# Row statistics of a layer norm inside a state-space scan: ScalarE accumulated sums in place of VectorE's statistics instructions

## The chip, the cores and the metric

The kernel runs as one program on one core of a Trainium2 chip. The metric is the device time of one launch in microseconds (us); lower is better. In the trace the engines are called PE (TensorE, with its weight loads as PEld), DVE (VectorE), ACT (ScalarE), POOL (GpSimd) and SP (SyncE, which only issues transfers here).

## What is computed

A two-layer network over 4096 tokens of width 256: graph convolution with a Mamba block, a mixture of experts, a second graph convolution, a second mixture of experts. Only the first graph convolution and its Mamba block are touched by the change:

```python
h = jax.nn.relu(adj @ x @ gcn_w + gcn_b)
mu = h.mean(-1, keepdims=True)
var = h.var(-1, keepdims=True)
h = (h - mu) * lax.rsqrt(var + EPS) * ln_g + ln_b      # the input norm
xz = h @ w_in                                          # 4096 x 1024: xc and z
u = silu(causal_conv4(xc)); dt, B, C from u            # 512 channels, 16 states
def step(hst, inp):                                    # over the 4096 tokens
    hst = dAt * hst + dBut
    return (hst, hst @ Ct)
y = (ys + u * D_skip) * silu(z);  out = y @ w_out
```

## The kernel before

**The scan stage.** The tokens are cut into 8 chunks of 512 (`CW`), a chunk into 4 tiles of 128 rows (`TPC`). The scan is written out by hand as 32 steps per chunk (`STEPS`); a step takes one block of 128 channels and two of the 16 states. The order in which the instructions are issued is each engine's order of execution; an engine never overtakes. In step n:

- POOL multiplies `db` for step n+1 (`inputs`, L1103) and then issues the accumulating transfer that adds the two halves of step n-1's `hc` (`pair`, L1132). `db` has two buffers, so the multiply for step n+1 needs step n-1's product on DVE and its state copy on ACT to be finished.
- DVE runs two scans (L1118), each on one decay `da` that ACT has made one step ahead (`decay`, L1111), and then the product `hc = db * cb` (L1128).
- ACT copies the last column of the state (L1124), and PE adds older `hc` into `psy` (L1145).

**The front of the next chunk.** From step 8 of chunk c on, the work ahead of chunk c+1's scan is slipped into the steps: `Front.PLAN` names what follows the product of a step, `Front.EARLY` what comes between the scans and the product. Chunk 0's front runs ahead of the scan, alone. The front's input norm is spread so:

| Step | Function | Engine and line before |
|---|---|---|
| 8 | `do_gcn` | PE L700 |
| 9 | `do_biased` | DVE adds the bias (L707), ACT takes the Relu, 128x512 at a time (L711) |
| 10, early | `do_stats` | DVE: four `bn_stats` (L715) and four `bn_aggr` (L716) |
| 10, early | `do_root` | DVE adds EPS (L719), POOL raises to the power -1/2 (L720) |
| 11 | `do_normal` | DVE makes `-mean * rstd` (L723), ACT normalises, four tiles (L727) |
| 12 | `do_turn` | PE transposes (L735) |
| 13 | `do_turned`, `do_xz` | ACT copies out with gain and bias (L742), PE multiplies by `w_in` (L754) |
| 17 | `do_silu` | ACT, after PE's convolution (L771), takes the Silu (L781) |

**The propagation pieces.** `adj @ x` for chunk c+2 (L642) is cut into 66 pieces per chunk (64 of matmuls, and two copies of the result, L648). A small loop ahead of the scan gives each step a number of pieces: it keeps an estimate of PE's time and of DVE's time per step (`PE_COST`, `DVE_COST`) and puts each next piece where PE's estimate is lowest against DVE's.

**The same statistics elsewhere.** While chunk 6 and 7 are scanned, `Tail.put` and `Tail.squares` take the row sums of the block's output by ACT: an Identity with a summed output (L905), the negated mean (L915) and a Square with the mean as bias and a summed output into `junk` (L919). `Norm.root` (L932, L935) and `Norm.shift` (L941) turn them into scale and shift.

Of the kernel before, what the change touches and what calls it, by code (L numbers as in the profile page):

```python
# [9 lines left out]
F32 = mybir.dt.float32  # L10
BF16 = mybir.dt.bfloat16
I32 = mybir.dt.int32
AF = mybir.ActivationFunctionType
ALU = mybir.AluOpType
# [4 lines left out]
P = 128  # L19
CW = 512  # L20
TPC = CW // P
TR = 256
EPS = 1e-5
# [5 lines left out]
def kernel(ctx: ExitStack, tc: tile.TileContext, out: bass.AP, **a):  # L29
    nc = tc.nc  # L30
    x, adj, adjT = a["x"], a["adj"], a["adjT"]
    N, D = x.shape
# [16 lines left out]
    small = ctx.enter_context(tc.tile_pool(name="small", bufs=3))  # L49
# [489 lines left out]
    with ExitStack() as s1:  # L539
# [51 lines left out]
        junk = ra.tile([P, D], F32, name="junk")  # L591
# [26 lines left out]
        FILL = {11: 8, 12: 2, 16: 1, 18: 2, 20: 2, 21: 6, 22: 1, 24: 40}  # L618
        PIECE, PE_STEP, DVE_STEP = 1.0, 1.1, 4.3
        PE_COST = {"gcn": 2, "turn": 0.8, "xz": 2, "conv": 4, "project": 2, "dt": 1}  # L620
        DVE_COST = {"biased": 0.8, "stats": 1.4, "soft": 2.7}
        psts, fronts = {}, {}
        
        def propagation(c):
# [27 lines left out]
        class Front:  # L652
# [3 lines left out]


            PLAN = {
                8: ["gcn 0", "gcn 1"], 9: ["biased 0", "biased 1"], 11: ["normal"],
                12: ["turn 0", "turn 1"], 13: ["turned 0", "turned 1", "xz 0", "xz 1"],  # L660
                14: ["in 0", "in 1", "xz 2"], 15: ["conv 0", "in 2"], 16: ["conv 1"],
                17: ["silu 0", "conv 2"], 18: ["xz 3"], 19: ["in 3", "project 0"],
# [4 lines left out]
                38: ["in 7"], 39: ["silu 2"],  # L667
            }
            EARLY = {
                10: ["stats 0", "stats 1", "root"], 27: ["soft 0"], 29: ["soft 1"],  # L670
                30: ["soft 2"], 31: ["soft 3"],
            }

            def __init__(self, c):
                self.c = c
                self.pts = psts.pop(c)
                self.h = w1p.tile([P, TPC, D], F32, name="h", tag="h")
                self.st = small.tile([P, TPC, 6], F32, name="ln_st")
                self.mv = small.tile([P, TPC, 2], F32, name="ln_mv")
                self.rs = small.tile([P, TPC], F32, name="ln_rs")  # L680
                self.nm = small.tile([P, TPC], F32, name="ln_nm")
                self.ps, self.psy = {}, {}
# [22 lines left out]
            def do_biased(self, hh):  # L705
                hs = self.h[:, 2 * hh:2 * hh + 2, :]
                nc.vector.tensor_tensor(  # L707
                    hs, self.ps.pop(("gcn", hh)), gcn_b.unsqueeze(1).to_broadcast([P, 2, D]),
                    ALU.add,
                )  # L710
                nc.scalar.activation(hs, hs, AF.Relu)  # L711

            def do_stats(self, hh):
                for t in range(2 * hh, 2 * hh + 2):
                    nc.vector.bn_stats(self.st[:, t, :], self.h[:, t, :])  # L715
                    nc.vector.bn_aggr(self.mv[:, t, :], self.st[:, t, :])  # L716

            def do_root(self):
                nc.vector.tensor_scalar(self.rs, self.mv[:, :, 1], EPS, None, ALU.add)  # L719
                nc.gpsimd.tensor_tensor(self.rs, self.rs, mhalf[:, :TPC], ALU.pow)  # L720

            def do_normal(self):
                nc.vector.scalar_tensor_tensor(  # L723
                    self.nm, self.mv[:, :, 0], -1.0, self.rs, ALU.mult, ALU.mult
                )
                for t in range(TPC):
                    nc.scalar.activation(  # L727
                        self.h[:, t, :], self.h[:, t, :], AF.Identity, bias=self.nm[:, t:t + 1],
                        scale=self.rs[:, t:t + 1],
                    )  # L730
# [425 lines left out]
        with tc.manual_schedule(engines={  # L1156
# [6 lines left out]
            for i, names in [*Front.PLAN.items(), *Front.EARLY.items()]:  # L1163
                for name in names:
                    pe[i % STEPS] += PE_COST.get(name.split()[0], 0.0)
                    dve[i % STEPS] += DVE_COST.get(name.split()[0], 0.0)
            pieces = [0] * STEPS
# [503 lines left out]
```

## Time and profile before

| | |
|---|---|
| Median of 3 runs | 2469.72 us (2467.38 to 2470.41) |
| The profiled execution, its own time | 2471.36 us |
| Its span, first to last instruction | 2469.6 us |
| Mean granted clock of PE | 0.955 |
| Busy share of the span: PE, DVE, ACT, POOL | 91%, 67%, 48%, 46% |
| The scans' first and last start | 168.7 us and 1288.7 us |

The span holds several stages one after the other: the first norm of x, chunk 0's propagation and front, the scan stage (some 1120 us), routing, the first experts, the second graph convolution, the second experts. The busy shares are means over all of them, so what a change inside the scan stage is worth is read from rows of that stage. In the timelines below a row gives start, duration, engine, line, operation, what it writes and reads, and, in brackets, how long the engine sat idle before it and who ended that.

### The profile page before, as it was taken

The page shows a single profiled execution, that of the slowest core. Times are in us where ns is not written, and L with a number is a line of the kernel's source. Part 1 is how long each engine was busy: PE and PEld are TensorE (multiplying, and loading weights), DVE is VectorE, ACT ScalarE, POOL GpSimd, SP SyncE. Part 2 cuts the span into 40 slices and gives each one's busy share as a digit, 9 for nine tenths or more (in the row PEclk, how much of TensorE's full clock was granted, in tenths as well). Part 3 has the DMA queues.
Part 4 walks back from the last instruction along what each step waited for, and adds up shares of the span by engine and source line. Part 5 has one row for each costly group of instructions (what it writes and reads, how often), then busy time and mean ns, then how long its engine had stood idle before and what let it go on. Part 6 is the DMA issues. An engine that isn't in the chain of part 4 may idle for free. (4 is left out here: it accounts for less than half of the span.)

```text
span 2469.6 us, 27703 instructions
## 1 busy us (share of the span) xinstructions
PE 2258.3 (91%) x8984; PEld 1635.7 (66%) x8984; DVE 1657.0 (67%) x2376; ACT 1180.8 (48%) x2013; POOL 1141.7 (46%) x830
## 2 busy tenths in 40 slices
PE   5989989999999989997994999969999999989985
PEld 4765655646565655643663888857788888878874
DVE  4049999999999999989897111165466666744233
ACT  1136657465655657466662322224555555633321
POOL 1027777687777677776551455410000000036652
PEclk9989999999999999997995999989999999999998
DMA  6359998989999999988655777643344444447886
GB/s 205 94 160 245 239 271 219 270 225 273 228 249 263 237 266 225 273 235 217 210 184 171 237 229 234 216 162 109 103 146 149 149 145 145 143 137 235 248 278 228
DMA packets 290364, 509.46 MB, mean 206 GB/s; under 512 B 25232, under 2 KB 157456, under 8 KB 289312
## 3 DMA queue, kind: packets, MB, share of 16 engines
q1 hardware_dynamic: 243936, 410.54, 53.2%
q0 software_dynamic: 46272, 97.03, 18.2%
q8 instruction: 75, 1.23, 0.2%
q14 instruction: 81, 0.66, 0.1%
HBM read 406.03 MB, written 42.73 MB: 182 GB/s over the span
## 5 line engine op out<-in xcount | busy, mean ns | idle before, releaser
L1103 POOL TENSOR_TENSOR db<-du,bb 128x1024 f32<-128x1024 f32 x256 | 607.2, 2372 | 357.5 <-ACT state L1124 130.0
L1118 DVE TENSOR_TENSOR_SCAN db<-da,state,db 128x512 f32<-128x512 f32 x512 | 627.2, 1266 | 44.6 <-ACT da L1111 42.3
L642 PE MATMUL pt<-at,gn 128*128 128x256 f32 x2048 | 489.6, 391 | 34.0 <-DMA at<-in_adjT_dram 27.1
L1111 ACT ACTIVATE da<-dt,negA 128x512 f32<-128x512 f32 x512 | 347.8, 691 | 357.0 <-DVE db L1118 355.3
L642 PEld LDWEIGHTS pt<-at,gn 128*128 128x128 f32 x2048 | 398.4, 196 | 164.0 <-issue 73.6
L1398 PE MATMUL pf<-gn,f 128*128 128x256 f32 x2048 | 452.0, 380 | 0.0
L1398 PEld LDWEIGHTS pf<-gn,f 128*128 128x128 f32 x2048 | 386.6, 190 | 57.2 <-issue 6.4
L1128 DVE TENSOR_TENSOR hc<-db,cb 128x1024 f32<-128x1024 f32 x256 | 331.4, 1294 | 17.9
L1145 PE MATMUL psy<-hc,ident 128*128 128x512 f32 x576 | 304.9, 622 | 41.9 <-DMA hc<-hc 33.4
L79 POOL TENSOR_TENSOR ln_rs<-ln_rs,mhalf 128x4 f32<-128x4 f32 x24 | 34.0, 1416 | 512.1 <-DVE ln_rs L78 512.1
L460 DVE TENSOR_TENSOR yk<-ps_y,bk 128x512 f32<-128x512 f32 x73 | 50.4, 691 | 326.5 <-PE ps_y L455 280.8
L1387 ACT ACTIVATE f<-f 128x1024 f32<-128x1024 f32 x128 | 134.5, 1057 | 197.8 <-DVE f L1386 133.8
L470 PE MATMUL ps_h<-xkT,wk 128*128 128x256 f32 x864 | 213.8, 389 | 11.7 <-DVE xkT L495 6.3
L455 PE MATMUL ps_y<-wk,hk 128*128 128x256 f32 x864 | 211.0, 381 | 0.1
L1132 POOL DMA_DIRECT2D hc<-hc x224 | 195.4, 873 | 0.2
L470 PEld LDWEIGHTS ps_h<-xkT,wk 128*128 128x128 f32 x864 | 160.2, 194 | 45.8 <-ACT hk L474 13.5
L1145 PEld LDWEIGHTS psy<-hc,ident 128*128 128x128 f32 x576 | 110.5, 198 | 120.3 <-issue 59.0
L1386 DVE TENSOR_SCALAR f<-at 128x1024 f32<-128x1024 f32 x128 | 88.1, 688 | 149.3 <-PE pf L1398 135.9
L455 PEld LDWEIGHTS ps_y<-wk,hk 128*128 128x128 f32 x864 | 161.6, 191 | 21.6 <-ACT hk L474 0.9
L474 ACT ACTIVATE hk<-ps_h,d_b 128x256 f32<-128x256 f32 x140 | 66.2, 474 | 184.0 <-PE ps_h L470 184.0
L1393 DVE SCALAR_TENSOR_TENSOR cnt<-at,cnt 128x1024 bf16<-128x1024 f32 x120 | 145.8, 1215 | 9.8 <-DMA at<-in_adjT_dram 8.9
L754 PE MATMUL ps_xz<-hT,w_in 128*128 128x512 f32 x256 | 124.9, 623 | 12.9 <-ACT hT L742 12.9
(305 smaller groups left out, 2568.8 us busy)
## 6 DMA issues: line engine op xcount, KB each, us to landing
at<-in_adjT_dram SPq DMA_DIRECT2D x256, 512.0 KB, 4.4
bb<-bcd SPq DMA_DIRECT2D x128, 512.0 KB, 5.1
cb<-bcd SPq DMA_DIRECT2D x128, 512.0 KB, 4.9
hc<-hc POOLq DMA_DIRECT2D x224, 256.0 KB, 6.7
wk<-in_L_ffn_W_dram SPq DMA_DIRECT2D x70, 512.0 KB, 5.2
wk<-in_L_ffn_expert_w_dram SPq DMA_DIRECT2D x114, 256.0 KB, 4.3
yg<-d_ys SPq DMA_DIRECT2D x16, 512.0 KB, 4.1
yd<-us SPq DMA_DIRECT2D x6, 1024.0 KB, 7.8
```

Source lines behind the costliest of these rows:

```text
L455: nc.tensor.matmul(ps[:, j, :], hT[:, m, j * P:(j + 1) * P], w[:, m, :], start=(m == 0), stop=(m == kb_out - 1),)
L470: nc.tensor.matmul(ps[:, j, :], w[:, d, m * P:(m + 1) * P], xT[:, d, :], start=(d == 0), stop=(d == DB - 1),)
L642: nc.tensor.matmul(pt[:, k, :], xl[:, j, k * P:(k + 1) * P], at[:, jj, :], start=(j == 0 and k == 0), stop=(j == NT - 1 and k == DB - 1),)
L1103: nc.gpsimd.tensor_tensor(self.db, self.f.du[self.half][:, self.mi:self.mi + 1, :].to_broadcast([P, 2, CW]), self.bb, ALU.mult,)
L1111: nc.scalar.activation(da, self.f.dt[self.half][:, self.mi, :], AF.Exp, scale=negA[:, self.m, n:n + 1])
L1118: nc.vector.tensor_tensor_scan(self.db[:, j, :], da, self.db[:, j, :], state[:, self.m, n:n + 1], ALU.mult, ALU.add,)
L1128: nc.vector.tensor_tensor(self.hc, self.db, self.cb, ALU.mult)
L1132: nc.gpsimd.dma_start(self.hc[:, 0, :], self.hc[:, 1, :], accum_op=ALU.add)
L1145: nc.tensor.matmul(f.psy[m], ident, self.hc[:, j, :], start=False, stop=(self.g == GS - 1 and j == last),)
L1387: nc.scalar.activation(f, f, AF.Square)
L1393: nc.vector.scalar_tensor_tensor(cnt, at, 0.0, cnt, ALU.is_gt, ALU.add)
L1398: nc.tensor.matmul(pf[:, t, :], f[:, jj, t * P:(t + 1) * P], gn[:, j, :], start=(j == 0 and t % 2 == 0), stop=(j == NT - 1 and t % 2 == 1),)
```

## The change

The variance and mean that `bn_stats` and `bn_aggr` made on DVE are made by summed outputs on ACT. `do_biased` splits its Relu into four, one per 128-row tile, each with a summed output into `nm`. `do_stats` moves from early in step 10 to the end of step 10: ACT turns the sums into negated means and takes four Squares with summed outputs into `rs`. `do_root` moves from early in step 10 to early in step 11, and its DVE instruction now also scales by 1/D. `do_normal` stays at the end of step 11; its DVE instruction becomes a plain multiplication of two tiles. The entry "stats" leaves `DVE_COST`; by the loop's arithmetic step 10 then gets 3 pieces of the propagation in place of 5, and steps 26 and 28 get 3 in place of 2.

```diff
-        DVE_COST = {"biased": 0.8, "stats": 1.4, "soft": 2.7}
+        DVE_COST = {"biased": 0.8, "soft": 2.7}
...
-                8: ["gcn 0", "gcn 1"], 9: ["biased 0", "biased 1"], 11: ["normal"],
+                8: ["gcn 0", "gcn 1"], 9: ["biased 0", "biased 1"], 10: ["stats"], 11: ["normal"],
...
             EARLY = {
-                10: ["stats 0", "stats 1", "root"], 27: ["soft 0"], 29: ["soft 1"],
+                11: ["root"], 27: ["soft 0"], 29: ["soft 1"],
...
-                self.st = small.tile([P, TPC, 6], F32, name="ln_st")
-                self.mv = small.tile([P, TPC, 2], F32, name="ln_mv")
...
-                nc.scalar.activation(hs, hs, AF.Relu)
-
-            def do_stats(self, hh):
                 for t in range(2 * hh, 2 * hh + 2):
-                    nc.vector.bn_stats(self.st[:, t, :], self.h[:, t, :])
-                    nc.vector.bn_aggr(self.mv[:, t, :], self.st[:, t, :])
+                    nc.scalar.activation(
+                        self.h[:, t, :], self.h[:, t, :], AF.Relu, accum_out=self.nm[:, t:t + 1]
+                    )
+
+            def do_stats(self):
+                nc.scalar.activation(self.nm, self.nm, AF.Identity, scale=-1.0 / D)
+                for t in range(TPC):
+                    nc.scalar.activation(
+                        junk, self.h[:, t, :], AF.Square, bias=self.nm[:, t:t + 1],
+                        accum_out=self.rs[:, t:t + 1],
+                    )

             def do_root(self):
-                nc.vector.tensor_scalar(self.rs, self.mv[:, :, 1], EPS, None, ALU.add)
+                nc.vector.tensor_scalar(self.rs, self.rs, 1.0 / D, EPS, ALU.mult, ALU.add)
                 nc.gpsimd.tensor_tensor(self.rs, self.rs, mhalf[:, :TPC], ALU.pow)

             def do_normal(self):
-                nc.vector.scalar_tensor_tensor(
-                    self.nm, self.mv[:, :, 0], -1.0, self.rs, ALU.mult, ALU.mult
-                )
+                nc.vector.tensor_tensor(self.nm, self.nm, self.rs, ALU.mult)
```

## The prediction

> **What bounds the kernel now.** I read the page's busy slices first, then the waits of the scan stage, then the timelines of steps 10 and 11 of one chunk. The slices:
>
> ```profile
> PE   5989989999999989997994999969999999989985
> DVE  4049999999999999989897111165466666744233
> ACT  1136657465655657466662322224555555633321
> ```
>
> In slices 3 to 20, the scan stage, PE and DVE are both at 9 and ACT at 4 to 7, so two engines could be the bound. The waits of DVE from 306 to 1152 us (six chunks) decide it:
>
> ```profile
> DVE db L1118 <- ACT da L1111: 29.0, 22, 2.8
> DVE us L1154 <- PE psy L1145: 3.9, 2, 2.1
> ```
>
> DVE waits 33 us in 846, and for PE hardly at all. A plain step is two scans and a product on DVE, and the next scan starts 3.68 us later (357.51 to 361.19 below). PE does idle: 0.70 us before the transposes of step 12 and 2.90 us before step 14's `xz` in this chunk. So DVE's queue sets the pace, and an instruction in it costs its full length. Steps 10, 11 and 12 of chunk 1, as the table of windows shows them (length first, then each engine's busy time):
>
> ```profile
> 347.31:353.12 5.81, 5.81 (x26) 4.63 (x25) 5.64 (x13) 2.23 (x5) 3.16 (x3) 1.00 1.04 246
> 353.12:357.51 4.39, 4.39 (x17) 2.87 (x16) 4.30 (x5) 1.50 (x3) 4.16 (x3) 1.00 0.92 282
> 357.51:361.19 3.68, 2.49 (x13) 1.72 (x13) 3.59 (x6) 3.39 (x7) 3.17 (x2) 1.00 0.84 215
> ```
>
> Step 10 is 2.13 us over a plain step, step 11 is 0.71 over. The timelines of DVE and POOL say why:
>
> ```profile
> 351.25 0.39 DVE L715 BATCH_NORM_STATS2 ln_st<-h 128x6 f32<-128x256 f32 x1
> 351.68 0.18 DVE L716 BATCH_NORM_AGGREGATE ln_mv<-ln_st 128x2 f32<-128x6 f32 x1
> 351.90 0.17 DVE L719 TENSOR_SCALAR ln_rs<-ln_mv 128x4 f32<-128x4 f32 x1
> 351.98 1.22 DVE L1128 TENSOR_TENSOR hc<-db,cb 128x1024 f32<-128x1024 f32 x1
> ...
> 355.66 1.85 DVE L1128 TENSOR_TENSOR hc<-db,cb 128x1024 f32<-128x1024 f32 x1
> ```
> ```profile
> 352.16 1.94 POOL L720 TENSOR_TENSOR ln_rs<-ln_rs,mhalf 128x4 f32<-128x4 f32 x1 [2.65 <-DVE ln_rs L719]
> 354.08 2.35 POOL L1103 TENSOR_TENSOR db<-du,bb 128x1024 f32<-128x1024 f32 x1
> ```
>
> The statistics fill step 10. The power delays POOL's `db` to 354.08; it ends at 356.43, and step 11's product, which reads two tiles as POOL's multiply does, takes 1.85 us in place of 1.22 and ends 1.08 after it. The power, too, needs 1.94 us beside a product (it ends 0.90 after the product's 353.20) and 1.01 us in chunk 0's front, where DVE is idle. So these two engines hold each other up, and the order in which they start counts.
>
> **The change, part by part.** I follow step 10 of chunk 1 with its scan's start as zero.
>
> *Removed from DVE:* eight instructions and the first `root`, in all 2.13 us. Step 10 falls from 5.81 to 3.68, and POOL's `db` for step 12 starts at 3.92 (product's end 3.76 plus 0.16, as in other steps) and ends at 6.26, before step 11's product: the 0.63 us of contention goes as well.
>
> *Added to ACT:* the rows of the same operations in the tail:
>
> ```profile
> 1062.62 0.21 ACT L915 ACTIVATE x_mean<-x_sum 128x2 f32<-128x2 f32 x1
> 1062.86 0.51 ACT L919 ACTIVATE junk<-xr,x_mean 128x256 f32<-128x256 f32 x1
> 1063.27 0.19 ACT L919 ACTIVATION_READ_ACCUMULATOR junk<-xr,x_mean 128x1 f32 x1
> 1063.49 0.51 ACT L919 ACTIVATE junk<-xr,x_mean 128x256 f32<-128x256 f32 x1
> ```
>
> A Square comes every 0.63 us, since the next writes the same `junk`. ACT's state copy of step 10 starts at 3.10 as before (the four Relus end near 1.3, where the decays first have to wait for a scan anyway). Then the mean at 3.19, Squares at 3.43, 4.06, 4.70 and 5.33, the last sum at 5.93. Queued behind them are the decays for step 12; the first could start at 4.96 and starts at 5.9. They end at 7.2 and are needed after 7.4: hidden, by 0.2 us if nothing else were late.
>
> *Moved: `root`.* On DVE it stands behind step 11's scans, at 6.04. The sums are there at 5.93, so no wait, but `db` is on POOL until 6.26; row L932, the same form, took 0.23 us in that place. The product then runs from 6.22 to 7.45. On POOL the power is moved past step 10's accumulating transfer, which holds POOL's queue for 0.87 us (6.24 to 7.12). It starts at 7.12 beside the product and ends 0.88 after it, at 8.33.
>
> *The new wait.* `normal`'s multiplication on DVE now waits for that power; behind it in DVE's queue stand step 12's scans, and so everything. DVE idles from 7.45 to 8.37. Worse, POOL's `db` for step 13 needs only step 11's product and state copy (7.27), so it starts as soon as the power is off POOL: at 352.16 + 1.94 = 354.10 against 354.08 above, 0.02 us before the power's end. DVE starts 0.04 after a power that it waits for (chunk 0's front: power at 92.99 for 1.01, L723 at 94.04). So `db` is first by some 0.05 us, and what a small DVE multiplication of two tiles does beside it, the last chunk shows:
>
> ```profile
> 1161.60 2.33 POOL L1103 TENSOR_TENSOR db<-du,bb 128x1024 f32<-128x1024 f32 x1
> ```
> ```profile
> 1161.75 2.21 DVE L941 TENSOR_TENSOR x_shift<-x_mean,x_dev 128x12 f32<-128x12 f32 x1
> ```
>
> It ends 0.03 after POOL's. So `nm` ends at 8.31 + 2.35 + 0.03 = 10.69, and step 12's scan starts at 10.61 (0.08 ahead of the end, as at 357.51). Steps 10 and 11 take 10.61 in place of 5.81 + 4.39 = 10.20: +0.41 us a chunk, for the seven chunks that carry a front +2.9 us. The bounds: with `nm` first, the scan starts at 8.33 + 0.04 + 0.15 - 0.08 = 8.44, or -1.76 a chunk (-12.3 in all); with the sums 0.5 us late, +0.9 a chunk (+6.4). Lateness is the smaller doubt; between the two orders the row at 0.15 us speaks for the blocked case, but it is a row at 0.15 and not at 0.05.
>
> The Trainium skill (SBUF — State Buffer, § Who interferes with whom) says that a VectorE instruction with two SBUF inputs and a GpSimd one that reads SBUF share an interface, that "Issue order, not op shape, decides who blocks", and that the loser waits for the whole instruction. The 2.21 us row agrees; the rule alone would give the blocked case, +2.9 us, and it speaks against this change.
>
> *Chunk 0's front* has nothing to hide behind. Today `nm` starts at 94.04, ACT normalises from 94.29 to 96.36, and PE, which has pieces until 96.5, loses nothing. The Relu of the second half starts at 90.55; as two with sums it lasts until 91.48 (0.42 from start to start: half of L711's 512 columns in 0.33, the sum 0.09), the mean until 91.72, the Squares until 94.22, `root` until 94.5, the power (1.01) until 95.5, `nm` until 95.7: ACT normalises from about 95.85, 1.55 us later. PE loses 1.15 of it, as the first transposes can start on the first tiles. PE then sets the way to the scan's start: +1.15 us (0.3 to 1.6).
>
> *The propagation pieces.* Two of the five leave step 10, and one each joins steps 26 and 28. A piece is four matmuls, 0.9 us. PE is up to 1.3 us later at the copy in step 28 where its idle time there is 0.46 us. ACT may wait that long, but the decays behind the copy are 3.9 us early in a step with the softplus work. PE catches up in step 2, where it waits 1.2 to 3.6 us for `hc`. I cost it at nothing; without that cover it is 1.3 us in three chunks, +4.
>
> *The sum:* -2.13 x 7 = -14.9 in step 10; step 11 from 4.39 to 6.93, +2.54 x 7 = +17.8; front 0 +1.15; together +4.1 us. The profiled execution, 2471.36, becomes 2475.4; the median of the runs is 1.64 below it, so 2473.8.
>
> **The rivals.** *`nm` gets in first.* The 0.05 us lie inside the gap that no row shows: -12.3 + 1.15 = -11.2, 2458.6 us. For it: POOL's power in its first 0.13 us does not yet collide (1.01 alone, 0.88 after a product), so its start is not quite its claim. Against: DVE's blocked product shows the same 0.15.
>
> *The granted clock of PE.* PE's idle time before the transposes grows from 0.70 to about 2.3 us, as it has two pieces less and `nm` comes no earlier. In chunk 1 the 2.90 us of idle time before `xz` cost it: the clock in 364 to 370 us is 0.73 and 0.70, the second Silu of step 18 waits for PE, and the step's scans start 5.80 us apart (379.67 and 385.47) against 4.29 in chunk 2, where the slow stretch fell elsewhere. Four of seven chunks pay this today (1, 3, 5, 6). If the other three pay too, +1.5 x 3 = +4.5, 2478.3 us. It decides when the clock is below 1 over `xz` in every chunk. The Trainium skill (TensorE: Matmul & The Clock Gate, Part 1) gives free-running windows of 3.4 us, of which an idle one halves the clock; a 2.3 us gap would by that rule be enough in some chunks and not in others, and the sum would lie between the two.
>
> *It makes no difference in the scan*, because PE would have held DVE back anyway: then only front 0 counts, 2470.9. The 3.9 us in the waits speak against it.
>
> **How the numbers follow.** Blocked `nm` 0.56, with a range of its own of 2470 to 2479 (sums late, clock by chance); `nm` first 0.25; clock 0.14; no difference 0.05. The measurement tells 0.2% (4.9 us) from no change: faster below 2464.8, slower above 2474.7. Of the blocked case I give 0.34 to the band and 0.22 above it. Faster 0.25; same 0.34 + 0.05 = 0.39; slower 0.22 + 0.14 = 0.36. The range must take in both signs to hold 8 in 10: 2457 to 2479.
>
> **What would show it.** Right: step 10 at 3.68 us, step 11 near 6.9, a DVE `nm` of over 2 us that ends with POOL's `db`, DVE idle about 0.9 us before it on POOL's `ln_rs`, the first scan about 1.2 us later than 168.7. Wrong: an `nm` of 0.15 us and step 11 near 4.8 (then faster); DVE waiting for ACT in front of `root` (then slower than said); steps 18 all at 5.8.

## The result and the profile after

The kernel before took 2470.06 us in the runs beside it (median of 6), the changed kernel 2485.01 us (median of 6, 2477.48 to 2489.13). The ratio is 1.0059, 95% interval [1.0044, 1.0075]: slower by 0.6%, where 2473.8 and at most 2479 were predicted. The profiled execution took 2485.26 us, 13.9 more than the profiled one before.

The same 40 slices of the changed kernel's page:

```profile
PE   5989989999999999987994999969999999989995
DVE  4049989999898999999897211166466666744233
ACT  1246657565665657466661322225455555533321
```

The scan stage looks as it did, PE and DVE at 9, and a slice of 62 us cannot show more. Its waits from 306 to 1152 us do (engine, line, what it waited for, then us in total, times, the longest):

```profile
DVE db L1120 <- ACT da L1113: 38.2, 24, 3.7
...
ACT pts L648 <- PE pt L642: 18.9, 10, 3.4
...
DVE ln_nm L727 <- POOL ln_rs L724: 5.6, 6, 0.9
```

The last row was foretold. The first two were not: DVE waits 9.2 us longer for the decays, and ACT's copy of the propagated rows (`pts`), which waited 1.9 us for PE before, now waits 18.9.

Steps 9 to 12 of chunk 1, in the table of windows (length, then busy time of PE, PEld, DVE, ACT, POOL, then the granted clock of PE):

```profile
345.51:350.78 5.27, 5.27 (x24) 4.28 (x23) 5.18 (x6) 2.61 (x8) 4.12 (x3) 1.00 0.78 203
350.78:354.39 3.61, 3.61 (x16) 2.80 (x16) 3.58 (x4) 3.02 (x12) 2.21 (x2) 1.00 0.92 253
354.39:361.32 6.93, 5.01 (x19) 3.02 (x17) 6.00 (x6) 3.53 (x11) 6.70 (x4) 1.00 1.05 240
361.32:365.00 3.68, 2.86 (x9) 1.98 (x10) 3.59 (x4) 3.38 (x7) 0.90 (x2) 0.59 0.70 169
```

Step 10 is a plain step and step 11 takes 6.93 us, in this chunk as in the other six. The timelines of POOL and DVE over step 11 show the block:

```profile
357.53 1.53 POOL L724 TENSOR_TENSOR ln_rs<-ln_rs,mhalf 128x4 f32<-128x4 f32 x1
359.05 2.33 POOL L1105 TENSOR_TENSOR db<-du,bb 128x1024 f32<-128x1024 f32 x1
```
```profile
356.94 1.23 DVE L1130 TENSOR_TENSOR hc<-db,cb 128x1024 f32<-128x1024 f32 x1
359.09 2.31 DVE L727 TENSOR_TENSOR ln_nm<-ln_nm,ln_rs 128x4 f32<-128x4 f32 x1 [0.93 <-POOL ln_rs L724]
```

DVE idles 0.93 us for the power; `db` starts 0.04 us before `nm`, and `nm`, four numbers a partition, lasts until `db` is done.

So steps 10 and 11 cost 10.55 us in place of 10.20, +2.4 us over seven chunks. The rest shows in the lengths of the other steps (from one step's first scan to the next one's). Step 8 took 5.41 us in four chunks before, 6.6, 6.2 and 5.9 in the others; now 5.41 in chunk 0, 7.0 in two and 7.44 in four, +8.8 us in all. Steps 5 and 6, 3.7 us each before, take about 4.4 and 4.06 in four chunks, +4.4. The two timelines of step 8 in chunk 1, ACT and then DVE, first those of the kernel before:

```profile
339.37 0.57 ACT L648 COPY pts<-pt 128x512 f32<-128x512 f32 x1
341.25 1.30 ACT L1111 ACTIVATE da<-dt,negA 128x512 f32<-128x512 f32 x2
```
```profile
342.04 2.46 DVE L1118 TENSOR_TENSOR_SCAN db<-da,state,db 128x512 f32<-128x512 f32 x2 [1.64 <-ACT da L1111]
```

and of the changed one:

```profile
337.84 1.28 ACT L780 ACT_TABLE_LOAD   x1
339.13 1.91 ACT L780 ACTIVATE zs<-zs 128x2048 f32<-128x2048 f32 x1
342.82 0.58 ACT L648 COPY pts<-pt 128x512 f32<-128x512 f32 x1 [1.77 <-PE pt L642]
343.42 1.28 ACT L1113 ACT_TABLE_LOAD   x1
344.72 1.30 ACT L1113 ACTIVATE da<-dt,negA 128x512 f32<-128x512 f32 x2
```
```profile
345.51 1.28 DVE L1120 TENSOR_TENSOR_SCAN db<-da,state,db 128x512 f32<-128x512 f32 x1 [3.67 <-ACT da L1113]
```

Before, the copy waited for nothing and DVE waited 1.64 us for the decays. Now the copy waits 1.77 us for PE's last piece, the table load and the decays stand behind it on ACT, and DVE waits 3.67 us for the decays. Why PE is late, PE's idle time before the pieces says, over the six chunks. First the kernel before, then the changed one (busy us, mean ns, then idle time before and who ended it):

```profile
L642 PE MATMUL pt<-at,gn 128*128 128x256 f32 x1344 | 327.2, 393 | 4.1 <-ACT pts L648 4.1
```
```profile
L642 PE MATMUL pt<-at,gn 128*128 128x256 f32 x1357 | 331.6, 392 | 25.0 <-DMA at<-in_adjT_dram 21.7 <-ACT pts L648 3.4
```

In these six chunks PE never waited for an adjacency block (`at`, a load that feeds four pieces); now it does for 21.7 us. SyncE's queue around the turn from chunk 0 to chunk 1, before:

```profile
294.37 0.32 SPq L1099 DMA_DIRECT2D cb<-bcd  x1
294.79 0.39 SPq L632 DMA_DIRECT2D at<-in_adjT_dram  x1
296.88 0.32 SPq L1099 DMA_DIRECT2D bb<-bcd  x1
297.86 4.70 SPq L632 DMA_DIRECT2D at<-in_adjT_dram  x2
306.18 0.34 SPq L1099 DMA_DIRECT2D cb<-bcd  x1
```

and after:

```profile
297.03 0.32 SPq L1101 DMA_DIRECT2D bb<-bcd  x1
297.44 1.08 SPq L632 DMA_DIRECT2D at<-in_adjT_dram  x2
306.34 0.34 SPq L1101 DMA_DIRECT2D cb<-bcd  x1
308.84 0.34 SPq L1101 DMA_DIRECT2D bb<-bcd  x1
309.27 0.39 SPq L632 DMA_DIRECT2D at<-in_adjT_dram  x1
```

The queue runs in order. Before, three `at` loads went out ahead of the `cb` load of 306 us, which waits for DVE's product, the first of them at 294.79; after, only two, from 297.44, and the third stands behind that `cb` load until 309.27, though the last matmul that read its buffer ended at 302.42. PE waits for `at` 2.62 us until 305.04 and 2.80 us until 316.73. SyncE is not among the four engines whose order the kernel writes by hand (`manual_schedule` names PE, DVE, ACT and POOL), so its queue is planned at build time, and the plan came out differently.

### The profile page after: what moved, and what is told of

The parts are those of the page before. It is cut to its first block, busy times and chain, and to the rows that moved or that the text cites. A ratio compares the mean times of both kernels' runs of the same rounds, so it can differ in the third digit from the quotient of the medians.

```text
span 2483.4 us, 27742 instructions
## 1 busy us (share of the span) xinstructions
PE 2264.7 (91%) x8984; PEld 1640.7 (66%) x8984; DVE 1653.4 (67%) x2312; ACT 1202.4 (48%) x2133; POOL 1135.2 (46%) x830
## 5 line engine op out<-in xcount | busy, mean ns | idle before, releaser
L1389 ACT ACTIVATE f<-f 128x1024 f32<-128x1024 f32 x128 | 134.6, 1057 | 196.3 <-DVE f L1388 132.0
L455 PEld LDWEIGHTS ps_y<-wk,hk 128*128 128x128 f32 x864 | 162.3, 192 | 21.7 <-ACT hk L474 0.9
L1395 DVE SCALAR_TENSOR_TENSOR cnt<-at,cnt 128x1024 bf16<-128x1024 f32 x120 | 145.8, 1215 | 10.8 <-DMA at<-in_adjT_dram 10.1
L1390 ACT ACTIVATE f<-f 128x1024 f32<-128x1024 f32 x128 | 134.5, 1055 | 3.4
```

The lines of the kernel that those rows point to most:

```text
L455: nc.tensor.matmul(ps[:, j, :], hT[:, m, j * P:(j + 1) * P], w[:, m, :], start=(m == 0), stop=(m == kb_out - 1),)
L1389: nc.scalar.activation(f, f, AF.Square)
L1395: nc.vector.scalar_tensor_tensor(cnt, at, 0.0, cnt, ALU.is_gt, ALU.add)
```

## The experiments

Three theories stood: the planned order of the loads makes TensorE late; the two moved pieces make it late by themselves; the new work on ScalarE sets the chunk back. The sets of runs fell on different chips, on which the kernel before took 2470.8 us (e1 to e4), 2473.1 (e5 to e8), 2489.8 (e9 to e11), 2497.6 (e12 to e15) and 2494.3 (e16 to e18). So ratios to the kernel before of the same set are what compares; step lengths hardly differ between chips.

**e1, the pieces back.**

```diff
             pe, dve = [PE_STEP] * STEPS, [DVE_STEP] * STEPS
+            dve[10] += 2.8
```

> The changed kernel with one part undone: step 10 of the piece plan is charged the 2.8 us of VectorE statistics again, so that the propagation pieces lie where they lay before (five in step 10, two each in steps 26 and 28) and the queue of loads falls back almost to its old order. The statistics stay on ScalarE. If the moved pieces, or the order of the loads that came with them, make step 8 longer (+8.8 us in all) and steps 5 and 6 (+4.4), these go: step 8 near 5.4 to 6.6, steps 10 and 11 still 3.6 and 6.9, 2470 + 2.4 = about 2472.5 us. If the new work on ScalarE or the blocked multiplication sets the chunk back by itself, the time stays at 2485.

2474.21 us, 1.0013 [1.0002, 1.0024]. TensorE waits for no `at`, step 8 is 5.4 to 6.65, steps 5 and 6 are 3.7, step 10 is 3.62 and step 11 6.93. TensorE's row for the pieces, in the six chunks:

```profile
L642 PE MATMUL pt<-at,gn 128*128 128x256 f32 x1363 | 336.9, 398 | 2.5 <-ACT pts L648 2.5
```

With the new work on ScalarE in place, steps 5 and 6 are as they were and step 8 is 2.0 us longer in all, where 8.8 had to be explained: that theory falls as the main cause, and what the 2.0 us come from was not tried. In the profiled executions steps 5, 6 and 8 take 11.2 us less than in the changed kernel, and the whole scan 7.3 less, because steps 15, 16 and 18 take 2.9 more; another 4.4 us of the difference lie behind the scan.

**e2, the moved pieces alone**, in the kernel before.

```diff
-        DVE_COST = {"biased": 0.8, "stats": 1.4, "soft": 2.7}
+        DVE_COST = {"biased": 0.8, "soft": 2.7}
```

> The kernel before with one part of the change alone: the statistics stay on VectorE, but step 10 of the piece plan is no longer charged for them, so that two pieces leave it for steps 26 and 28. If pieces or loads are the cause, step 8 is 7.0 to 7.4 us in four or five chunks and the time 2479 to 2483 us. If the cause is the statistics on ScalarE, it stays at 2470 (2468 to 2473).

2482.05 us, 1.0044 [1.0029, 1.0058]. Step 8 is 6.5 to 7.45 in six chunks, with steps 10 and 11 as before (5.81 and 4.39), and TensorE waits 16.1 us for `at`:

```profile
L642 PE MATMUL pt<-at,gn 128*128 128x256 f32 x1362 | 336.8, 396 | 19.5 <-DMA at<-in_adjT_dram 16.1 <-ACT pts L648 3.4
```

One deleted entry of a cost table, without any other change, makes the kernel 0.4% slower.

**e3, `nm` on GpSimd.**

```diff
                 nc.gpsimd.tensor_tensor(self.rs, self.rs, mhalf[:, :TPC], ALU.pow)
+                nc.gpsimd.tensor_tensor(self.nm, self.nm, self.rs, ALU.mult)

             def do_normal(self):
-                nc.vector.tensor_tensor(self.nm, self.nm, self.rs, ALU.mult)
```

> The changed kernel with the multiplication nm = nm * rs on GpSimd, right behind the power, in place of VectorE. The pieces and the order of the loads are those of the changed kernel. If the prediction's reading of step 11 holds (VectorE waits 0.9 us for the power and is then blocked 2.3 us by GpSimd's db), step 11 falls from 6.93 by 1.5 to 2.9 us in seven chunks: -10 to -20, 2465 to 2475 us, with step 8 still at 7.0 to 7.4. If the time lost in step 11 only hides a later wait (TensorE behind its loads), step 11 falls but steps 5 to 8 take it back, and the time stays within 4 us of 2485.

2469.64 us, 0.9995 [0.9985, 1.0004]; 15.4 under the changed kernel. Its windows of steps 10 to 12 in chunk 1:

```profile
346.02:349.64 3.62, 3.62 (x16) 2.81 (x16) 3.59 (x5) 3.02 (x12) 2.20 (x2) 1.00 0.72 226
349.64:353.32 3.68, 3.68 (x17) 2.71 (x15) 3.68 (x5) 3.52 (x11) 3.46 (x3) 1.00 0.75 206
353.32:357.89 4.57, 3.01 (x15) 1.81 (x14) 4.48 (x4) 3.27 (x7) 4.33 (x4) 1.00 0.92 253
```

Steps 11 and 12 take 8.25 us in place of 10.61, and the multiplication costs GpSimd 0.20 us. What stays is `db`, later by power and multiplication, which then overlaps step 12's product. Steps 8 are still 7.2 to 7.4 in six chunks, as said.

**e4, `cb` on another queue.**

```diff
-                        nc.sync.dma_start(t, self.f.bcd[r0:r0 + 2, :].partition_broadcast(P))
+                        (nc.scalar if t is self.cb else nc.sync).dma_start(
+                            t, self.f.bcd[r0:r0 + 2, :].partition_broadcast(P))
```

> The changed kernel with the cb loads issued from ScalarE's queue, so that the loads of the adjacency (at) no longer stand behind a cb load that waits for VectorE's product. Pieces and all else as in the changed kernel. If the blocked loads are the cause, TensorE no longer waits for at, step 8 falls to 5.4 to 6.2 and the time to 2472 to 2477 us. If it is the place of the pieces themselves, whatever the loads do, step 8 stays near 7 and the time at 2483 to 2487. If ScalarE's issuing costs more than is hidden, the decays come late in every second step.

2491.16 us, 1.0086 [1.0068, 1.0104]. Step 8 is 5.41 in all seven chunks, but this settles nothing: `cb` now comes late (products wait 23.6 us for it, step 6 takes 5.9 to 7.0 in six chunks), which gives TensorE time, and TensorE still waits 15.8 us for `at`, now behind `bb`.

**e5, e3 and e1 together.**

> Both edits at once: nm on GpSimd behind the power, and the pieces back in their old steps. If the two costs are independent, as the steps of the first four runs say (old pieces: 2485.0 to 2474.2, -10.8; nm on GpSimd: -15.4), they add up: 2485.0 - 26.2 = about 2459 us (2456 to 2462), steps 8 at 5.4 to 6.6, steps 10, 11 and 12 at 3.6, 3.7 and 4.6, and the kernel is faster than the one before by 0.45%. If one hides behind the other, it is 2466 to 2470.

2455.30 us, 0.9930 [0.9913, 0.9946]: 17.8 us faster than the kernel before. The two costs add up: the ratios of e1 and e3 against the changed kernel's give 0.9949, and the measured one lies a little under that, as does e18's below (0.9940).

**e6, e7 and e8, all `bb` and `cb` loads on ScalarE's queue**, two steps ahead, in the changed kernel, in the one before, and with `nm` on GpSimd.

```diff
+            def load(self):
+                bb = w2p.tile([P, 2, CW], F32, name="bb")
+                cb = w2p.tile([P, 2, CW], F32, name="cb")
+                for t, r0 in ((bb, 2 * self.g), (cb, NS + 2 * self.g)):
+                    nc.scalar.dma_start(t, self.f.bcd[r0:r0 + 2, :].partition_broadcast(P))
+                ahead.append((bb, cb))
...
+                if cur.mi == 0 and i < STEPS - 2:
+                    Step(*divmod(n + 2, STEPS)).load()
```

> The changed kernel with both the bb and the cb loads issued from ScalarE's queue, two steps ahead of their use, so that SyncE's queue has hardly anything but the at loads and nothing in it waits for VectorE or GpSimd. The pieces lie as in the changed kernel. If the order of the loads is the cause of the late TensorE, its waits for at (21.7 us in six chunks) go to under 3, step 8 is 5.4 to 6.2 with steps 5 and 6 at 3.7, and the time about 2472 to 2476, if the 32 issues a chunk on ScalarE are hidden. If it is the place of the pieces, step 8 stays near 7 though at comes in time, 2483 to 2487. The run e4 did not tell this, since there TensorE still waited 15.8 us for at, behind bb.

> The kernel before with the same move of the bb and cb loads: what the move itself costs. If its issues are hidden, 2468 to 2472 us, steps 8 at 5.4 to 6.0. Beside e6: if the order of the loads is the cause, e6 is 0 to 5 us over this one (steps 10 and 11 alone, +2.4); if the place of the pieces is, 10 to 15 us.

> nm on GpSimd and the loads apart, with the pieces of the changed kernel. If the loads are the cause: 15 to 17 us under e6, about 2457 to 2460. If the place of the pieces is the cause: 2466 to 2471.

2733.07, 2712.44 and 2703.20 us: 1.1054, 1.0977 and 1.0925. A failed set. On ScalarE's queue the issues stand behind decays that wait for scans, and `bb` comes late: in e6 GpSimd waits 176 us for it in the six chunks. With such losses in nearly every second step the pair says nothing on step 8.

**e9, e10 and e11, SyncE's queue by hand**, in the changed kernel, in the one before, and in e5's. SyncE is added to `manual_schedule`, and `at`, `bb` and `cb` are issued ahead of their use. What the expectations call pieces ahead are `at` loads ahead.

> The changed kernel with SyncE's queue in an order written out by hand instead of one that is planned: every at load two pieces ahead of its use, bb and cb in the step after the product that frees their buffer, so that little in that queue stands behind a wait. The pieces lie as in the changed kernel. If the order of the loads is what makes TensorE late, its waits for at (21.7 us in six chunks) fall under 4, step 8 is 5.4 to 6.6, steps 5 and 6 are 3.7, and the time 2470 to 2476 us. If the place of the pieces is the cause by itself, step 8 stays at 7.0 to 7.4 with at in time, 2481 to 2487.

> The kernel before with the same rule for SyncE's queue: what that rule itself costs or brings. 2467 to 2474 us, step 8 at 5.4 to 6.6, TensorE waiting under 4 us for at. Beside e9: e9 is 0 to 5 us over this run if the order of the loads was the cause (steps 10 and 11 alone give +2.4), 10 to 15 us if the place of the pieces was.

> nm on GpSimd, the pieces in their old steps, and SyncE's queue by hand. Against e5 (2455.3) only the order of the loads differs. If the planned order of e5 still costs something in steps 8 (5.2 to 6.7, 5.4 without a wait: some 4 us in all), it is 2451 to 2455 us; if the order by hand is itself worse, 2456 to 2465.

2553.72, 2555.76 and 2541.68 us: 1.0266 [1.0247, 1.0285], 1.0271 [1.0243, 1.0299] and 1.0201 [1.0173, 1.0230]. e9 and e10 are level, no `at` is waited for in e9 and its step 8 is 5.41 in five chunks; but steps 23, 27 and 29 lost 7 us a chunk, because an `at` load two ahead waits for the last of the three buffers (the queue waits 337 us for pieces in six chunks, 71 before), and `bb` behind it. That, too, gave TensorE time.

**e12 and e13, a third `cb` buffer** (and four of `hc` for five), in the changed kernel and in the one before.

```diff
-                    self.cb = w2p.tile([P, 2, CW], F32, name="cb")
+                    self.cb = w2p.tile([P, 2, CW], F32, name="cb", bufs=3)
...
-                self.hc = w2p.tile([P, 2, CW], F32, name="hc", bufs=5)
+                self.hc = w2p.tile([P, 2, CW], F32, name="hc", bufs=4)
```

> The changed kernel with a third buffer for cb (paid for with the fifth buffer of hc), so that a cb load waits for a product two steps earlier and the at loads behind it come sooner, with the pieces as in the changed kernel. If the blocked loads make TensorE late, its waits for at fall from 21.7 us to under 8, step 8 to 5.4 to 6.6, and the time is 0 to 5 us over e13. If the place of the pieces does it, step 8 stays above 7 and the time is 10 to 15 us over e13.

> The kernel before with a third buffer for cb and four for hc: what that edit itself costs or brings. Within 4 us of the kernel before if the fifth hc buffer was never needed; 5 to 20 us slower if the products have to wait for TensorE.

2512.29 and 2499.83 us: 1.0067 [1.0044, 1.0089] and 1.0007 [0.9988, 1.0025]. The edit did not do what it was meant to: the queue was planned anew and e12's TensorE waits 25.0 us for `at`, products 43 us for a free `hc`. It tells nothing against either theory.

**e14 and e15, the order by hand, second form**: at most one `at` load ahead, `bb` a step earlier, `cb` after the product that frees its buffer. The edit, cut to its core, in the changed kernel (e14) and in the one before (e15):

```diff
-                    at = adp.tile([P, 4, HW], F32, name="at")
-                    nc.sync.dma_start(at, ...)
+                    while len(ats) < 2 and todo:
+                        fetch_at()
+                    at = ats.pop(0)
...
-            mybir.EngineType.Pool,
+            mybir.EngineType.Pool, mybir.EngineType.SP,
...
+                if n + 2 < NC * STEPS:
+                    if cur.mi == 0:
...
+                        load_c((fr if i == STEPS - 2 else fronts[c]).bcd, (i + 2) % STEPS // 2 % GS)
                 if nxt is not None:
                     nxt.inputs(cur)
+                if n + 3 < NC * STEPS and cur.mi == 1:
+                    load_b((fr if i == STEPS - 3 else fronts[(n + 3) // STEPS]).bcd, (i + 3) % STEPS // 2 % GS)
```

> The changed kernel with SyncE's queue by hand, second form: at one piece ahead instead of two (so that the queue does not stand still behind an at load whose buffer TensorE still reads, as it did for 13 us in e9), bb a step earlier. Pieces as in the changed kernel. If the loads are the cause: TensorE waits under 5 us for at, step 8 is 5.4 to 6.6, steps 23, 27 and 29 are back at 4.1, 6.3 and 5.9, and the time is 0 to 5 us over e15. If the place of the pieces is: step 8 above 7, 10 to 15 us over e15.

> The kernel before with the second order by hand: the base for e14. 2 us under to 15 us over the kernel before, steps 23, 27 and 29 at 4.1, 6.3 and 5.9 if bb now comes in time.

2497.27 and 2499.42 us: 1.0005 [0.9990, 1.0020] and 1.0013 [0.9999, 1.0027]. Under one rule for the loads the change makes no difference that can be measured. e14's row for the pieces, in the six chunks, and its windows of steps 10 and 11 of chunk 1:

```profile
L650 PE MATMUL pt<-at,gn 128*128 128x256 f32 x1364 | 332.0, 392 | 4.2 <-ACT pts L656 3.4 <-DMA at<-in_adjT_dram 0.8
```
```profile
351.90:355.52 3.62, 3.62 (x16) 2.81 (x16) 3.59 (x4) 3.02 (x12) 2.21 (x2) 1.00 0.93 248
355.52:362.45 6.93, 5.28 (x19) 2.94 (x17) 6.00 (x7) 3.52 (x11) 6.70 (x4) 1.00 1.05 291
```

The waits for `at` are down to 0.8 us, steps 5 and 6 are 3.7, step 8 is 5.41 in five chunks and 6.6 to 6.7 in two, and no step of chunks 0 to 5 gives TensorE time that it had not before, but for 2.9 us in steps 15 to 18 of chunk 4; the moved pieces and the blocked `nm` are still there. This is the test that e4, e6 and e9 were meant to be: the moved pieces do not make TensorE late by themselves, the order of the loads made the difference. Two things about the pair belong beside it. In e15, with the pieces in their old steps, TensorE waits 8.3 us for `at`, so this order suits the moved pieces better than the old ones. That the times are level owes something to step 18: e14 spends 3.0 us more than e15 in steps 10 and 11 and 4.4 less in step 18.

**e16, e17 and e18, the place of the pieces with `nm` on GpSimd**: e14 with `nm` on GpSimd, the same with the old pieces, and e5 again.

> e14 (the pieces of the changed kernel, SyncE's queue by hand in its second form) with nm on GpSimd. Without the late loads nothing else should take back what steps 11 and 12 give: 15 to 18 us under e14, which was level with the kernel before (1.0005), so a ratio of 0.993 to 0.995 and the same time as e5's edits. If part of e5's gain came from the old pieces beyond the order of the loads, it is 0.996 to 0.999.

> nm on GpSimd, the pieces in their old steps, and SyncE's queue by hand in its second form. If the order by hand is as good as the planned one of e5, 0.992 to 0.995; faster than e16 by over 0.1% only if the old steps suit TensorE better whatever the loads do.

> The edits of e5 once more, on the chip of e16 and e17, as the base for these two: 0.992 to 0.995 of the kernel before.

2486.02, 2488.05 and 2481.17 us: 0.9967 [0.9954, 0.9980], 0.9971 [0.9956, 0.9986] and 0.9940 [0.9918, 0.9961]. e16 and e17 are level, so the old place of the pieces brings nothing that the times show. Their profiled executions differ: step 8 is 6.5 to 7.0 in four chunks of e16 and 6.4 or more in two of e17, and the scans of e16 last 1114.6 us, those of e17 1106.7. With DVE 2.4 us a chunk faster TensorE has less to spare; whether that is the pieces, or the chance of one execution, stays open. `nm` on GpSimd gave 0.4% on e14, some 10 us, where 15 to 18 were expected: steps 11 and 12 gave their 16.9, but step 8, at 6.5 to 7.0 in four chunks against two, and step 18, at 5.2 to 5.8 in five chunks where e14 had one such, took some of it back. The kernel of e5 is the best of all, in both of its runs.

## Why the prediction was wrong

*Step 10, right.* 5.81 us were to become 3.68; it became 3.62 in all chunks. The Squares came in time: in the seven chunks DVE does not wait for ACT at L723 (in chunk 0's front, where nothing hides them, it waits 3.80 us).

*Step 11, right, and by the mechanism named.* 6.93 us were predicted and 6.93 measured. The wait for the power was put at 0.92 us and was 0.93, the order of `db` and `nm` at 0.05 us apart and was 0.04, `nm` at 2.32 (from 8.37 to 10.69) and it took 2.31. The power began 0.37 us sooner than forecast and took 1.53 us in place of 1.21, but it ended 0.89 after the product, as the prediction had it (0.88). e3 shows the price: without wait and block, 2.36 us a chunk come back. The Trainium skill (SBUF — State Buffer, § Who interferes with whom) has the loser wait for the whole instruction, and a lead of 0.04 us sufficed for that here.

*Chunk 0's front, not confirmed.* ACT normalises from 96.16 in place of 94.29, 1.87 later (1.55 predicted), and PE's `xz` starts at 100.61 in place of 99.13, 1.48 later. But the first scan starts at 168.52 in place of 168.69: the term of +1.15 shows as -0.17. PE did not set the way to it as the prediction had it, or one execution hides it: in e2, whose front is the old one, the first scan starts at 169.75, in e1 and e3 at 168.91 and 167.66. How the lateness of `xz` was made good was not tried.

*The propagation pieces, the step that failed.* The prediction costed the moved pieces "at nothing; without that cover it is 1.3 us in three chunks, +4". It asked where PE's work goes and what hides it, and the cover that it named holds where loads come in time, though PE is later than the 1.3 us that it gave: in e14 the copy of step 28 waits 1.8 to 3.5 us for PE in five of six chunks, and steps 28 and 29 keep their lengths. (In e2 the copy waits 5.0 us in two chunks, and there steps 29 and 30 are 0.8 us longer.) What it did not ask is what the moved pieces do to the queue that feeds them. Each fourth piece needs an `at` load, SyncE's order is planned from the others' work, and the new plan put `at` loads behind `cb` loads that wait for DVE. Steps 5, 6 and 8 became 13.2 us longer, and putting the pieces back (e1) takes 11.2 of them away, or 10.8 in the median of the whole: nearly three times the bound of +4 that was given. The prediction followed the pieces on PE alone; every queue that a moved step draws on had to be followed as well. Here the order on SyncE was seen in the traces; whether it can be had before a run was not tried.

*The sum.* From the first step to the last the scan came out 11.5 us longer: +2.4 from steps 10 and 11, +8.8 from step 8, +4.4 from steps 5 and 6, -3.2 from step 18 (luck, as the clock below shows) and -0.9 in chunk 7; what other steps add nearly cancels. It starts 0.2 us sooner. The last 2.5 us of the profiled difference lie behind the scan, where one execution differs from the next: from the last step's first scan to the span's end the profiles of before, e1, e2, e3 and e5 take 1182.1, 1180.2, 1179.2, 1180.8 and 1181.4 us, that of the changed kernel 1184.6.

*The rivals.* `nm` first did not happen in any of the seven chunks. The clock rival failed in its sign: step 18 is at 5.8 or more in two chunks where it was in four. The longer idle time before the transposes (1.98 us in chunk 1, 0.70 before) goes with a slower PE: the granted clock is halved for 6.8 us around steps 12 and 13 in six of the seven chunks, and in the other twice for 3.4, where before it was 3.4 us in six. But this stretch now comes early enough to be over when `xz` starts: steps 12, 13 and 14 of chunk 1 have a clock of 0.59, 0.50 and 0.99, before 1.00, 1.00 and 0.57. In chunks 0 to 5 step 18 is long in just those chunks whose clock is below 1 over `xz`: 1, 3 and 5 before, 3 now. (Chunk 6, which the prediction counted with them, has a clock of 1.00 over `xz` in both.) Nor do the prediction's words on idle windows fit the trace: a gap of 2.3 us fills no window of 3.4, yet in chunk 1 the half clock starts at 362.0, after 3.4 us in which PE worked for 1.10. "No difference in the scan" falls with e3, where the 16.5 us that DVE saved in steps 11 and 12 reached the end of the kernel (-15.4).

## What to carry to other kernels

A number in a planner's cost table is a change to the kernel: before an edit is costed, compare the order of every queue in the two programs (here the traces showed it), above all of those that nobody orders by hand, and for each load that moved ask what it now stands behind. A queue that runs in order and mixes loads with early and late conditions makes the early ones as late as the late ones. A result of a few numbers that a slower engine has just made is best finished there: VectorE paid 0.93 us of waiting and 2.31 us of blocking for a multiplication that GpSimd did in 0.20.

## What was not expected of the hardware

The same program's time differs between chips by about 1%: the kernel before had medians from 2470.8 to 2497.6 us in the five sets, while steps of the scan in which nothing is waited for hold their lengths to 0.01 us (3.68 for a plain step in the runs of every set). The traces show where it lies: from the last step's first scan to the end of the span, work in which no edit changed anything, the profiles of the first set and of e1 to e8 take 1176 to 1185 us, those of e9 to e18 1194 to 1212. Loads are not issued for nothing on a busy engine: a `bb` or `cb` issue in ScalarE's queue took 0.33 and 0.49 us in the pair that was looked at, and moving all 256 there cost 240 us (e7), with GpSimd waiting for `bb` 42 times, 171 us, in the 192 steps of the six chunks; how much of it is the issues themselves was not tried.
